# Channel stage of a four-layer convolution block: row-pair spectra, two-bank PSUM tiles and shorter Toeplitz rows

## The chip, the cores and the metric

The kernel runs on one core of one Trainium2 chip. The metric is device time of the whole launch in microseconds. All data are 32-bit floats; the trace shows each such matrix product as two instructions on TensorE (PE), each with a weight load of its own (PEld).

## The reference

The input x holds 32 images of 192 channels and 56 by 56 pixels. Four layers follow each other, each of the form x = x + layer(groupnorm(x)), with groups of 6 channels: an agent attention, a linear recurrence over the pixels (scan), a learned shift by whole pixels with a 3 by 3 filter, and a long convolution with a 55 by 55 filter for each channel. Cut to the two last ones, which the change touches:

```python
def _L2_conv_ref(inp, offset):          # a shift, then a separable 3x3 filter
    ...
    out = jax.vmap(shift_one, in_axes=(1, 0, 0, 0), out_axes=1)(x, yc, xc, mask)
    kern = jnp.exp(-sq / (2.0 * SIGMA ** 2))
    out_LO = jax.lax.conv_general_dilated(out, kern, ..., feature_group_count=Cn)

def _L3_conv_ref(x, z, ...):            # filter k from sines, then a long convolution
    ...
    y = jnp.fft.irfft2(jnp.fft.rfft2(x, s) * jnp.fft.rfft2(k[0], s)[None], s)
    y = y[..., Kh // 2:Kh // 2 + H, Kw // 2:Kw // 2 + W]
    return y + bias * x

x = x + _L2_conv_ref(_gn(x), L2_conv_offset)
x = x + _L3_conv_ref(_gn(x), ...)
```

## The kernel before, in words

`all_blocks` runs four parts in turn: `make_filter` (the long filter and its spectra along x, written to memory as `lags`), `attention` with `copy_spans` beside it (which lays the spectra out as `spans`), `scan_pairs`, and `channel_blocks`. Only the last, the channel stage, is touched.

The channel stage works on one channel at a time, all 32 images of it: a tile `x` has 112 used partitions, 56 image rows for each of two half batches that start at partitions 0 and 64, and 16 images by 56 columns along the free dimension. The steps of a channel c are:

- `load` (SP queue): two DMAs of x. `norm` (POOL): scale and shift of the first group norm; every fourth channel also builds the small matrices of the shift.
- `move_rows`, `move_columns` (PE): 8 products each, with the rows' and columns' matrices. Between them ACT copies the result into `across`; after them DVE adds it into x and sums it (`sums`).
- For a group of 6 channels `find_mean` and `find_spread` (small PE products), `keep_mean` (DVE). `centre` (DVE) and `square` (ACT), `sum_squares` (DVE) belong to a channel 6 behind c.
- `analyse` (PE), for a channel 12 behind: `_rows_to_spectra` multiplies 128 rows (both half batches) by `f1`, which holds cosines and sines for each half in a block of its own; 8 products of 168 columns, 3 to a PSUM tile. ACT copies the results to `y` in pieces of 64 partitions.
- `convolve` (PE): for each of 42 frequencies u, y against `toep`, the channel's Toeplitz matrix, 128 partitions by 56 by 84. Four products lie beside each other in 32-column strips of the array; 11 rounds of four make 44 products, the last two repeat u = 41. ACT writes the result into `turned`, scaled by the group's `rs`.
- `turn` (DVE): a transposition into `z`. `synthesise` (PE): 4 products with `back`. `finish` (DVE): two additions into `done`, and two DMAs on SP's queue to the output, in pieces of 224 bytes.
- `load_toeplitz` (ACT's queue): one DMA of 2352 KB, 128 partitions by 7 column groups of 2688 bytes each, asked for after `convolve` of channel b and meant for b + 3; there are three `toep` tiles.

The order is written out by hand in the loop at the end of `channel_blocks`. Each engine is wrapped in `_InOrder`, so every instruction of the stage carries the helper's line, L1546, in the profile, and stands on its engine in the order of the source. In one turn of the loop PE runs move_rows of channel c + 1, the group's mean and spread where they are due, analyse of b + 1, move_columns of c, synthesise of e = b - 1, and convolve of b, with b = c - 12. DVE's order in a turn is: the spreads' sums, turn (z), keep_mean, centre, the addition of move_columns, its sum, the addition of finish, the sum of squares. ACT's order is: the copy to across, the copies to y, square, the writes of turned, the issue of the Toeplitz load.

All PSUM tiles of the stage come from one pool of 8 tiles of one bank, taken in turn.

The scan, which is not changed, has two lines that the prediction uses: L921 multiplies by weights of 128 rows and L924 by weights of 64 rows, alternating between partitions 0 to 63 and 64 to 127:

```python
for h in range(len(outs[0])):
    for t, r in enumerate((slice(0, 64), slice(64, 128))):
        mm(outs[t][h], ca[r], srcs[2][h][r], start=False, stop=True)
```

Of the kernel before, what the change touches and what calls it, by code (L numbers as in the profile page):

```python
# [30 lines left out]
S = 56  # L31
# [1518 lines left out]
def channel_blocks(ctx: ExitStack, tc: tile.TileContext, taps, k, x2, rs2, spans, out):  # L1550
# [8 lines left out]
    nc = tc.nc  # L1559
    NB = out.shape[0]  # L1560
    NI, NG = NB // 2, NB // 4
    PX = 8 * S
    cp = ctx.enter_context(tc.tile_pool(name="d_c", bufs=1))
    wp = ctx.enter_context(tc.tile_pool(name="d_w", bufs=2))
    sp = ctx.enter_context(tc.tile_pool(name="d_s", bufs=2))
    pp = ctx.enter_context(tc.tile_pool(name="d_p", bufs=8, space=PSUM))
    pe, vector, scalar, pool, sync = (_InOrder(tc, e) for e in (nc.tensor, nc.vector, nc.scalar, nc.gpsimd, nc.sync))
    mm = pe.matmul

# [4 lines left out]
    pieces, at = [], 0  # L1574
# [80 lines left out]
    def load_toeplitz(c):  # L1655

        if not 0 <= c < C:
            return
        t = toep[c % len(toep)].rearrange("p j f -> p (j f)")
        n = S // SPAN  # L1660
        first = spans[c * n * 128]
        there = bass.AP(first.tensor, first.offset, [[FREQ, 128], [128 * FREQ, n], [1, SPAN * FREQ]])
        scalar.dma_start(out=t.rearrange("p (q f) -> p q f", q=n), in_=there)

    def move_rows(c):

        xn, rows = normed.pop(c).rearrange("p g w -> p (g w)"), made[c // 4][0]
        moved = across[c % len(across)]
        for i in range(0, NG, 4):
            ps = psum()  # L1670
            for g in range(4):
                mm(
                    ps[: 2 * S, g * 2 * S : (g + 1) * 2 * S], xn[:, (i + g) * 2 * S : (i + g + 1) * 2 * S], rows,
                    start=True, stop=True,
                )
            scalar.copy(
                moved[:, i : i + 4, :, 0:S].rearrange("p g s h -> p (g s) h"),
                ps[: 2 * S, :PX].rearrange("p (n h) -> p n h", h=S),
            )
        return moved  # L1680

    def move_columns(c, moved):

        n, j = divmod(c, GROUP)
        cols, x = made[c // 4][1], xs[c % len(xs)]
        flat = x.rearrange("p g w -> p (g w)")
        for i in range(2):
            ps = psum()
            for g in range(4):
# [22 lines left out]

    def find_mean(q):

        ps = psum()
# [8 lines left out]

    def find_spread(q):
        q.rs = sp.tile([128, 1], F32, name="rs", tag="rs")
        ps = psum()
# [16 lines left out]
        vector.tensor_reduce(groups[n].sums[:, 1, j], sq, AX.X, ALU.add)  # L1744

    def analyse(c):
        y = wp.tile([128, NI, 2, NF], F32, name="y", tag="y")
        _rows_to_spectra(pe, scalar, psum, padded[c % len(padded)], f1, y, NG)
        return y.rearrange("p g s u -> p (g s) u")

    def convolve(c, y):

        q, o, t = groups[c // GROUP], turned[c % len(turned)], toep[c % len(toep)]
        if c % GROUP < len(turned):
            vector.tensor_copy(o[0:32, :, SLOTS], q.fill.to_broadcast([32, S]))
        for a0 in range(0, QUAD, 4):
            n = min(4, QUAD - a0)
            ps = psum()
            for a in range(n):
                for i in range(4):  # L1760
                    u = min(4 * (a0 + a) + i, NF - 1)
                    mm(
                        ps[32 * i : 32 * i + 32, a * 2 * S : (a + 1) * 2 * S], y[:, :, u], t[:, :, 2 * u : 2 * u + 2],
                        start=True, stop=True,
                    )
            scalar.activation(
                o[:, :, 2 * a0 : 2 * (a0 + n)].rearrange("p j (a m) -> p a j m", m=2),
                ps[:, : n * 2 * S].rearrange("p (a j m) -> p a j m", a=n, m=2),
                AF.Copy, scale=q.rs,
            )  # L1770

    def turn(c):
        z = wp.tile([128, 32, S], F32, name="z", tag="z", bufs=1)
# [3 lines left out]
    def synthesise(c, z):  # L1777

        by = z.rearrange("p (g s) j -> p s g j", s=2)
        got = []  # L1780
        for i in range(2):
            ps = psum()
            for s in range(2):
                mm(
                    ps[HALF * s : HALF * s + HALF, :PX].rearrange("p (g w) -> p g w", w=S), back,
                    by[:, s, 8 * i : 8 * i + 8], start=True, stop=True,
                )
            got.append(ps[:, :PX].rearrange("p (g w) -> p g w", w=S))
        return got

    def finish(c, got):
        y = wp.tile([128, NI, S], F32, name="done", tag="done")
        t = padded[c % len(padded)][:, :, 0:S][:, :, ::-1]
        for i in range(2):
            g = slice(8 * i, 8 * i + 8)
            vector.tensor_tensor(y[:, g], t[:, g], got[i], ALU.add)
# [208 lines left out]
```

## Time and profile before

| | us |
|---|---|
| median of 3 timed runs | 10363.48 (10363.17 to 10363.57) |
| profiled execution | 10372.07 |
| its span, first to last instruction | 10370.2 |
| the channel stage in it | from about 8243 to 10370 |
| TensorE busy | 9436.8 (91%) |
| VectorE (DVE) busy | 9099.9 (88%) |
| ScalarE (ACT) busy | 6324.4 (61%) |

The page cuts the span into 40 slices and gives the busy tenths of each engine; the last 8 slices are the channel stage. Matrix products overlap in the pipeline, so a busy TensorE is not one at its peak, and how long a step takes is better read from start to start. The mean granted TensorE clock is 0.962 of full speed over the span and full in the steady part of the channel stage.

### The profile page before, as it was taken

Reading aid. Unit: us, or ns where it says so; the run is one execution under the profiler, and the core shown is the slowest. Engines: PE = TensorE matmul, PEld = TensorE weight load, DVE = VectorE, ACT = ScalarE, POOL = GpSimd, SP = SyncE. Lnnn points to the kernel's source line nnn. Section 1 sums busy time; section 2 is a strip of 40 time slices with the busy share of each in tenths; the row PEclk is TensorE's granted clock in tenths of the full one; section 3 lists DMA queues with packets and bytes.
Section 4 is the critical chain, followed back from the end, with each engine's and each line's share of the span. In section 5 each row is a group of like instructions: output and inputs, shape, how many; then the busy total and the mean of one; then the engine's idle time right before and its main releaser. Section 6 shows DMA issues by size and latency. Waiting matters only on the chain. (4 is left out here: it accounts for less than half of the span.)

```text
span 10370.2 us, 162899 instructions
## 1 busy us (share of the span) xinstructions
PE 9436.8 (91%) x63814; PEld 5816.8 (56%) x63814; DVE 9099.9 (88%) x11284; ACT 6324.4 (61%) x11964; POOL 2223.2 (21%) x1751
## 2 busy tenths in 40 slices
PE   5999999999999999998888888888888799999998
PEld 3555555655565555555333343333334488888886
DVE  5888888888888888887999999999999788888887
ACT  3555555555555555554566666666666567777777
POOL 0000000000000000000333333333333354554442
PEclk9999999999999999998899999999999899999999
DMA  4212221122112211111244444344444489999999
GB/s 129 68 37 66 68 68 44 58 68 68 47 55 68 68 46 29 49 49 43 69 107 101 103 103 105 104 104 101 101 101 101 129 247 303 307 306 304 304 304 278
DMA packets 1111096, 1247.61 MB, mean 120 GB/s; under 512 B 773091, under 2 KB 813440, under 8 KB 1098232
## 3 DMA queue, kind: packets, MB, share of 16 engines
q1 hardware_dynamic: 914284, 746.65, 28.1%
q10 hardware_dynamic: 196036, 490.46, 13.9%
q8 instruction: 506, 8.29, 0.3%
q14 instruction: 270, 2.21, 0.1%
HBM read 916.15 MB, written 306.43 MB: 118 GB/s over the span
## 5 line engine op out<-in xcount | busy, mean ns | idle before, releaser
L649 DVE SCALAR_TENSOR_TENSOR o<-v_a,att_w,o 128x896 f32<-128x896 f32 (+1 forms) x1024 | 1056.8, 1032 | 422.2 <-ACT v_a L623 301.9
L1167 POOL MEMSET f<- 128x2 f32 x48 | 4.5, 99 | 4751.2 <-DMA st_c<-st 4748.8
L1546 DVE STREAM_TRANSPOSE z<-turned 128x1792 f32<-128x1792 f32 x192 | 680.3, 3543 | 211.2 <-ACT turned L1546 211.2
L1546 ACT COPY y<-ps 64x252 f32<-64x252 f32 (+1 forms) x2304 | 784.6, 341 | 89.6 <-PE ps L1546 59.8
L1161 ACT ACTIVATE pq<-pq 128x784 f32<-128x784 f32 x384 | 329.4, 858 | 676.6 <-DVE pq L1157 676.4
L1153 DVE TENSOR_TENSOR_SCAN pq<-decay,f,both 128x784 f32<-128x784 f32 x384 | 695.7, 1841 | 9.1 <-ACT both L1183 9.1
L1157 DVE SCALAR_TENSOR_TENSOR pq<-both,eu,pq 128x1568 f32<-128x1568 f32 x384 | 701.3, 1840 | 2.0 <-POOL f L1156 0.4
L666 ACT ACTIVATE pr<-ps,low 98x896 f32<-98x896 f32 (+1 forms) x384 | 352.3, 918 | 572.7 <-DVE low L664 572.7
L1153 DVE TENSOR_TENSOR_SCAN pq<-decay,b,both 128x784 f32<-128x784 f32 x384 | 694.1, 1839 | 0.0
L921 PE MATMUL ps<-x,weights 128*128 128x392 f32 x1536 | 584.6, 519 | 83.4 <-ACT x L1141 54.2
L649 DVE SCALAR_TENSOR_TENSOR o<-v_c,att_w,o 128x448 f32<-128x448 f32 (+1 forms) x1024 | 638.6, 624 | 4.9
L662 PE MATMUL ps<-xs_a,gk_a 128*98 128x448 f32 (+1 forms) x1536 | 636.8, 495 | 0.0
L776 ACT ACTIVATE pq<-pq 128x1176 f32<-128x1176 f32 (+2 forms) x224 | 241.9, 1080 | 642.5 <-DVE pq L768 620.5
L663 PE MATMUL ps<-xs_c,gk_c 125*98 125x448 f32 (+1 forms) x1536 | 631.3, 492 | 0.0
L1141 ACT ACTIVATE x<-x,nb,rs 128x784 f32<-128x784 f32 x384 | 386.5, 1030 | 337.3 <-DMA x<-x 183.2
L1546 PEld LDWEIGHTS ps<-toep,y 128*32 128x32 f32 x16896 | 500.4, 151 | 160.9 <-issue 76.0
L763 PE MATMUL ps<-gq_a,xs_a 128*128 128x294 f32 (+1 forms) x1600 | 547.0, 425 | 37.7 <-DVE pq L768 33.1
L1546 PE MATMUL ps<-toep,y 128*32 128x112 f32 x16896 | 560.5, 286 | 12.6 <-DVE done L1546 11.1
L1156 POOL COPY b<-pq 128x2 f32<-128x2 f32 x192 | 394.7, 2056 | 660.9 <-DVE pq L1153 567.3
L1546 POOL TENSOR_TENSOR xn<-x,scale 128x896 f32<-128x896 f32 x192 | 329.7, 1717 | 937.4 <-DMA x<-x 670.5
L764 PE MATMUL ps<-gq_c,xs_c 125*128 125x294 f32 (+1 forms) x1600 | 519.9, 413 | 0.0
L1546 ACT ACTIVATE turned<-ps,rs 128x448 f32<-128x448 f32 (+1 forms) x576 | 377.3, 663 | 223.3 <-PE ps L1546 216.0
(360 smaller groups left out, 23488.2 us busy)
## 6 DMA issues: line engine op xcount, KB each, us to landing
toep<-spans ACTq DMA_DIRECT2D x192, 2352.0 KB
x<-x SPq DMA_DIRECT2D x576, 392.0 KB
x<-x SPq DMA_DIRECT2D x896, 196.0 KB
out_x<-done SPq DMA_DIRECT2D x384, 196.0 KB
spans<-lags SPq DMA_DIRECT2D x24, 2352.0 KB
x<-in_x SPq DMA_DIRECT2D x32, 1568.0 KB
x<-x SPq DMA_DIRECT2D x32, 1568.0 KB
gq_c<-once SPq DMA_DIRECT2D x32, 821.1 KB
```

Source lines behind the costliest of these rows:

```text
L649: nc.vector.scalar_tensor_tensor(dst, tap(i), dww[:, t, i : i + 1], dst, ALU.mult, ALU.add)
L662: mm(ps[P2, h, :n], g[:, cols], xs_a[j][:, px], start=True, stop=False)
L663: mm(ps[P2, h, :n], gk_c[0:KC, 2 * j + h, cols], xs_c[j][0:KC, px], start=False, stop=True)
L666: nc.scalar.activation(pr[:, :, :n], ps[P2, :, :n], AF.Exp, bias=low[:, j, p : p + 1], accum_out=sums[:, j, p : p + 1])
L763: mm(ps[:m, k - q, :HA], xs_a[j][:, px], g, start=True, stop=False)
L764: mm(ps[:m, k - q, :HA], xs_c[j][0:KC, px], gq_c[0:KC, which[k]], start=False, stop=True)
L921: mm(out, aa, srcs[t][h], start=True, stop=False)
L1141: nc.scalar.activation(xs[t], xs[t], AF.Identity, bias=nb1[:, t, s.p : s.p + 1], scale=rs1[:, t, s.p : s.p + 1])
L1153: nc.vector.tensor_tensor_scan(to, decay[:, of(t)].to_broadcast([128, MC]), data, at[:, i : i + 1], ALU.mult, ALU.add)
L1156: nc.gpsimd.tensor_copy(at, z[:, :, last])
L1157: nc.vector.scalar_tensor_tensor(before, both, eu[:, of(t)], before, ALU.mult, ALU.add)
L1546: return lambda *args, **kw: self.tc.keep_in_program_order(do(*args, **kw))
```

## The change

Five things change in `channel_blocks`:

1. `analyse` no longer calls `_rows_to_spectra`. For each of the 8 image pairs it makes two products of 64 rows, one for each half batch, of 84 columns, into two banks of one tile. Six pairs go into a first tile and two into a second; ACT copies 56 partitions at a time.
2. All PSUM tiles are two banks wide, and there are 4 of them. The results of move_rows, move_columns and synthesise lie in one tile each, and ACT or DVE reads both banks in one instruction. convolve has two tiles (64 and 20 instructions on PE).
3. convolve makes 42 products and not 44; move_columns uses 120 of 128 weight columns.
4. `load_toeplitz` fetches the three middle column groups as before, on ACT's queue, and the outer four in four DMAs on SP's queue, 48 partitions and 5376 bytes each. The rows left out are zeros, written once.
5. `toep`, `y` and `turned` are zeroed in part at the start of the stage.

```diff
+    ROWS = HALF + S
-    pp = ctx.enter_context(tc.tile_pool(name="d_p", bufs=8, space=PSUM))
+    pp = ctx.enter_context(tc.tile_pool(name="d_p", bufs=4, space=PSUM))
...
+    EDGE = 8
+    for t in toep:
+        for p in (0, HALF):
+            nc.vector.memset(t[p : p + 32, 0 : 2 * SPAN], 0.0)
+            nc.vector.memset(t[p + 32 : p + 64, 0 : 2 * SPAN], 0.0)
+            nc.vector.memset(t[p + 32 : p + 64, 5 * SPAN :], 0.0)
...
+        nc.vector.memset(t[64:128, :, SLOTS - 2 : SLOTS], 0.0)
+    ys = kept("y", [128, NI, 2, NF], 2)
+    for t in ys:
+        nc.vector.memset(t, 0.0)
...
-        return pp.tile([128, BANK], F32, name="ps", tag="ps")
+        return pp.tile([128, 2, BANK], F32, name="ps", tag="ps")
...
-        there = bass.AP(first.tensor, first.offset, [[FREQ, 128], [128 * FREQ, n], [1, SPAN * FREQ]])
-        scalar.dma_start(out=t.rearrange("p (q f) -> p q f", q=n), in_=there)
+        there = bass.AP(
+            first.tensor, first.offset + 2 * 128 * FREQ, [[FREQ, 128], [128 * FREQ, 3], [1, SPAN * FREQ]]
+        )
+        scalar.dma_start(out=t.rearrange("p (q f) -> p q f", q=n)[:, 2:5], in_=there)
+        for q, p, to in ((1, EDGE, 0), (5, 0, 5)):
+            for m in range(2):
+                there = bass.AP(
+                    first.tensor, first.offset + (q * 128 + m * HALF) * FREQ, [[FREQ, S - EDGE], [1, 2 * SPAN * FREQ]]
+                )
+                at = HALF * m + p
+                sync.dma_start(out=t[at : at + S - EDGE, to * SPAN * FREQ : (to + 2) * SPAN * FREQ], in_=there)
...
-        for i in range(2):
-            ps = psum()
-            for g in range(4):
-                mm(ps[:, g * 2 * S : (g + 1) * 2 * S], moved[:, 4 * i + g].rearrange("p s h -> p (s h)"), cols[: 2 * S], start=True, stop=True)
-            px = slice(i * PX, (i + 1) * PX)
-            vector.tensor_tensor(flat[:, px], flat[:, px], ps[:, :PX], ALU.add)
+        ps = psum()
+        for g in range(NG):
+            mm(
+                ps[:ROWS, g // 4, g % 4 * 2 * S : (g % 4 + 1) * 2 * S],
+                moved[:, g].rearrange("p s h -> p (s h)")[:, :ROWS], cols[: 2 * S], start=True, stop=True,
+            )
+        there = x[:ROWS].rearrange("p (b g) w -> p b (g w)", b=2)
+        vector.tensor_tensor(there, there, ps[:ROWS, :, :PX], ALU.add)
...
-        y = wp.tile([128, NI, 2, NF], F32, name="y", tag="y")
-        _rows_to_spectra(pe, scalar, psum, padded[c % len(padded)], f1, y, NG)
+        y, flat = ys[c % len(ys)], padded[c % len(padded)].rearrange("p g w -> p (g w)")
+        for g0, n in ((0, 6), (6, 2)):
+            ps = psum()
+            for g in range(n):
+                at = (g0 + g) * 128
+                for s in range(2):
+                    r = slice(HALF * s, HALF * s + HALF)
+                    mm(
+                        ps[:ROWS, s, g * FREQ : (g + 1) * FREQ], flat[r, at : at + ROWS],
+                        f1[r, s * FREQ : (s + 1) * FREQ], start=True, stop=True,
+                    )
+            got = ps[:, :, : n * FREQ].rearrange("p s (g m u) -> p s g m u", m=2, u=NF)
+            for i in range(2):
+                for m in range(2):
+                    scalar.copy(
+                        y[HALF * m : HALF * m + S, 2 * g0 + i : 2 * (g0 + n) : 2].rearrange("p g s u -> p s g u"),
+                        got[HALF * i : HALF * i + S, :, :, m],
+                    )
...
-        for a0 in range(0, QUAD, 4):
-            n = min(4, QUAD - a0)
+        for a0, n in ((0, 8), (8, QUAD - 8)):
             ps = psum()
             for a in range(n):
-                for i in range(4):
-                    u = min(4 * (a0 + a) + i, NF - 1)
+                for i in range(min(4, NF - 4 * (a0 + a))):
+                    u = 4 * (a0 + a) + i
...
+            for p, part in ((128, slice(0, n - 1)), (64, slice(n - 1, n))):
+                scalar.activation(
+                    o[:p, :, 16:SLOTS].rearrange("p j (a m) -> p a j m", m=2)[:, part],
+                    ps[:p, 0, : n * 2 * S].rearrange("p (a j m) -> p a j m", a=n, m=2)[:, part],
+                    AF.Copy, scale=q.rs[:p],
+                )
```

move_rows, synthesise and finish change in the same way as move_columns: one tile, one copy or addition over both banks. The first eight rounds of convolve are written to `turned` in one instruction of ACT.

More of the change, by code (lines that the diff above doesn't have):

```diff
@@ L1668, in move_rows @@
         moved = across[c % len(across)]
-        for i in range(0, NG, 4):
-            ps = psum()
-            for g in range(4):
[L1672 to L1678, printed above, removed]
-            )
+        ps = psum()
+        for g in range(NG):
+            mm(
+                ps[: 2 * S, g // 4, g % 4 * 2 * S : (g % 4 + 1) * 2 * S], xn[:, g * 2 * S : (g + 1) * 2 * S], rows,
+                start=True, stop=True,
+            )
+        scalar.copy(
+            moved[:, :, :, 0:S].rearrange("p (b g) s h -> p b (g s) h", b=2),
+            ps[: 2 * S, :, :PX].rearrange("p b (n h) -> p b n h", h=S),
+        )
         return moved
@@ L1685, in move_columns @@
         cols, x = made[c // 4][1], xs[c % len(xs)]
-        flat = x.rearrange("p g w -> p (g w)")
-        for i in range(2):
-            ps = psum()
-            for g in range(4):
-                mm(ps[:, g * 2 * S : (g + 1) * 2 * S], moved[:, 4 * i + g].rearrange("p s h -> p (s h)"), cols[: 2 * S], start=True, stop=True)
-            px = slice(i * PX, (i + 1) * PX)
-            vector.tensor_tensor(flat[:, px], flat[:, px], ps[:, :PX], ALU.add)
+        ps = psum()
+        for g in range(NG):
+            mm(
[4 more added lines that the diff above has]
+        vector.tensor_tensor(there, there, ps[:ROWS, :, :PX], ALU.add)
         if j == 0:
@@ L1713, in find_mean @@
     def find_mean(q):
-        ps = psum()
+        ps = psum()[:, 0]
         mm(ps[:, :NI], ones, q.total, start=True, stop=True)
@@ L1726, in find_spread @@
         q.rs = sp.tile([128, 1], F32, name="rs", tag="rs")
-        ps = psum()
+        ps = psum()[:, 0]
         for i in range(4):
@@ L1746, in analyse @@
     def analyse(c):
-        y = wp.tile([128, NI, 2, NF], F32, name="y", tag="y")
-        _rows_to_spectra(pe, scalar, psum, padded[c % len(padded)], f1, y, NG)
+        y, flat = ys[c % len(ys)], padded[c % len(padded)].rearrange("p g w -> p (g w)")
+        for g0, n in ((0, 6), (6, 2)):
+            ps = psum()
+            for g in range(n):
+                at = (g0 + g) * 128
+                for s in range(2):
+                    r = slice(HALF * s, HALF * s + HALF)
+                    mm(
+                        ps[:ROWS, s, g * FREQ : (g + 1) * FREQ], flat[r, at : at + ROWS],
[4 more added lines that the diff above has]
+                for m in range(2):
+                    scalar.copy(
+                        y[HALF * m : HALF * m + S, 2 * g0 + i : 2 * (g0 + n) : 2].rearrange("p g s u -> p s g u"),
+                        got[HALF * i : HALF * i + S, :, :, m],
+                    )
         return y.rearrange("p g s u -> p (g s) u")
@@ L1755, in convolve @@
             vector.tensor_copy(o[0:32, :, SLOTS], q.fill.to_broadcast([32, S]))
-        for a0 in range(0, QUAD, 4):
-            n = min(4, QUAD - a0)
+        for a0, n in ((0, 8), (8, QUAD - 8)):
             ps = psum()
             for a in range(n):
-                for i in range(4):
-                    u = min(4 * (a0 + a) + i, NF - 1)
-                    mm(
-                        ps[32 * i : 32 * i + 32, a * 2 * S : (a + 1) * 2 * S], y[:, :, u], t[:, :, 2 * u : 2 * u + 2],
-                        start=True, stop=True,
-                    )
[L1766 to L1770, printed above, removed]
+                for i in range(min(4, NF - 4 * (a0 + a))):
+                    u = 4 * (a0 + a) + i
+                    mm(
+                        ps[32 * i : 32 * i + 32, a // 4, a % 4 * 2 * S : (a % 4 + 1) * 2 * S], y[:, :, u],
+                        t[:, :, 2 * u : 2 * u + 2], start=True, stop=True,
+                    )
+            if a0 == 0:
+                scalar.activation(
+                    o[:, :, 0:16].rearrange("p j (b a m) -> p b a j m", b=2, m=2),
+                    ps[:, :, :PX].rearrange("p b (a j m) -> p b a j m", a=4, m=2),
+                    AF.Copy, scale=q.rs,
+                )
+                continue
+            for p, part in ((128, slice(0, n - 1)), (64, slice(n - 1, n))):
+                scalar.activation(
+                    o[:p, :, 16:SLOTS].rearrange("p j (a m) -> p a j m", m=2)[:, part],
+                    ps[:p, 0, : n * 2 * S].rearrange("p (a j m) -> p a j m", a=n, m=2)[:, part],
+                    AF.Copy, scale=q.rs[:p],
+                )
     def turn(c):
@@ L1779, in synthesise @@
         by = z.rearrange("p (g s) j -> p s g j", s=2)
-        got = []
+        ps = psum()
         for i in range(2):
-            ps = psum()
             for s in range(2):
                 mm(
-                    ps[HALF * s : HALF * s + HALF, :PX].rearrange("p (g w) -> p g w", w=S), back,
+                    ps[HALF * s : HALF * s + HALF, i, :PX].rearrange("p (g w) -> p g w", w=S), back,
                     by[:, s, 8 * i : 8 * i + 8], start=True, stop=True,
                 )
-            got.append(ps[:, :PX].rearrange("p (g w) -> p g w", w=S))
-        return got
+        return ps[:, :, :PX].rearrange("p b (g w) -> p b g w", w=S)
     def finish(c, got):
@@ L1793, in finish @@
         t = padded[c % len(padded)][:, :, 0:S][:, :, ::-1]
-        for i in range(2):
-            g = slice(8 * i, 8 * i + 8)
-            vector.tensor_tensor(y[:, g], t[:, g], got[i], ALU.add)
+        vector.tensor_tensor(
+            y.rearrange("p (b g) w -> p b g w", b=2), t.rearrange("p (b g) w -> p b g w", b=2), got, ALU.add
+        )
         for s in range(2):
```

## The prediction

> **What bounds it now.** I read the slices of the page first: the edit touches only the last stage, from 8243 us to the end, and there DVE, PE and DMA are all near full. The windows view of 400 us of that stage gives the totals (columns: stretch, length, busy PE, weight loads, DVE, ACT, POOL, granted clock, DMA share, GB/s), and the DMA view of the same stretch splits the DMA share by queue (q10 carries ACT's issues, the Toeplitz loads; q1 carries SP's).
>
> ```profile
> 9200.00:9600.00 400.00, 394.52 (x5483) 335.25 (x5483) 349.81 (x352) 306.64 (x696) 200.58 (x175) 1.00 1.02 306
> q10 hardware_dynamic: 34510, 91.13, 65.9%
> q1 hardware_dynamic: 75345, 30.42, 35.3%
> ```
>
> The groups count 38 transposes in it, so a channel takes 400/38 = 10.53 us: DVE works 9.2, ACT 8.1, DMA 10.7 by the sum of its packets. Which of PE and DMA sets the pace? The timeline of PE tells it (start, length, instructions): a group's first channel, then an ordinary one.
>
> ```profile
> 9291.33 1.20 PE L1546 MATMUL ps<-toep,y 128*32 128x112 f32 x32
> ...
> 9301.85 1.72 PE L1546 MATMUL ps<-z,fixed 128*64 128x448 f32 x8 [0.83 <-DVE x L1546]
> 9303.50 2.86 PE L1546 MATMUL ps<-toep,y 128*32 128x112 f32 x88
> 9306.29 1.82 PE L1546 MATMUL ps<-rows,xn 128*112 128x112 f32 x16
> 9307.95 2.46 PE L1546 MATMUL ps<-fixed,padded 128*128 128x168 f32 x16
> 9310.25 1.94 PE L1546 MATMUL ps<-cols,across 112*128 112x112 f32 x16
> 9312.11 1.73 PE L1546 MATMUL ps<-z,fixed 128*64 128x448 f32 x8
> 9313.77 2.52 PE L1546 MATMUL ps<-toep,y 128*32 128x112 f32 x76
> ```
>
> From start to start the ordinary channel costs: convolve 2.79, move_rows 1.66, analyse 2.30, move_columns 1.86, synthesise 1.66: 10.27 us with no wait between them. Over the stage five channels of six take 10.27 to 10.4; the group's first takes 11.3 to 12.7 (here 12.17), for DVE is late and PE waits for its PSUM. So TensorE is the bound of the ordinary channel. The Toeplitz load asked for after convolve of channel b is for b+3 and in the trace lands some 12 us after its issue; no PE wait in the waits view names it. DMA is the second limit, close behind.
>
> **PE, step by step.** Analyse swaps 8 products of 128 rows by 168 columns (two instructions each, 16 in all, 142 ns apart) for 16 products of 64 rows by 84 columns, in pairs on the two halves of the array's rows. Nothing in this stage does that, but the scan's L924 does, between full products of L921 (PEld is the weight load):
>
> ```profile
> 8217.01 0.96 PEld L924 LDWEIGHTS ps<-sq,fixed 64*128 64x128 f32 x8 [0.56 <-issue]
> 8217.01 1.59 PE L924 MATMUL ps<-sq,fixed 64*128 64x392 f32 x8
> 8218.53 2.27 PEld L921 LDWEIGHTS ps<-y,wogs 128*128 128x128 f32 x8 [0.56 <-issue]
> 8218.53 2.90 PE L921 MATMUL ps<-y,wogs 128*128 128x392 f32 x8
> 8221.36 0.96 PEld L924 LDWEIGHTS ps<-y,wogs 64*128 64x128 f32 x8 [0.56 <-issue]
> ```
>
> Start to start, 8 full ones take 2.83 and 8 half ones 1.52. If halves run two at a time, 8s + w = 2.83 and 4s + w = 1.52, so a step s is 0.33 us (392 columns) and a change of shape w is 0.21 us; the loads' busy time falls by the same half, so they overlap too. In analyse a pair streams only 84 columns, half of today's 142 ns, so the load of 120 columns will set the step: 112-column loads go 98 ns apart (1.66/16 with its change of shape), 128-column loads in move_columns 111. I take 104 ns. Analyse: 16 x 0.104 = 1.66, plus 0.21 at each end, which today's neighbours of equal shape don't pay: 2.08 instead of 2.30.
>
> [...]
>
> Move_columns loads 120 columns for 128: 16 x 7 ns = 0.10 less, 1.76. Convolve drops two repeated products (88 instructions to 84, 2.79/22 = 0.127 per four; the last fours become half-filled and save less): 0.05 less, 2.74. Move_rows and synthesise keep their instructions. Sum: 1.66 + 2.08 + 1.76 + 1.66 + 2.74 = 9.90, so 0.37 us less per ordinary channel. Bounds: pairs at 98 and no drain, 0.9 less; pairs at 208, nothing overlapped, 1.3 more.
>
> **ACT and DVE.** Rows of ACT in the groups of the same stretch (after the count: busy us, mean ns of one; then the idle time before):
>
> ```profile
> L1546 ACT COPY y<-ps 64x252 f32<-64x252 f32 x304 | 110.6, 364 | 14.6 <-PE ps L1546 11.1
> L1546 ACT ACTIVATE turned<-ps,rs 128x448 f32<-128x448 f32 x76 | 54.0, 718 | 39.9 <-PE ps L1546 39.1
> L1546 ACT COPY y<-ps 64x168 f32<-64x168 f32 x152 | 44.7, 294 | 2.2
> L1546 ACT ACTIVATE turned<-ps,rs 128x336 f32<-128x336 f32 x38 | 21.2, 559 | 0.5
> ```
>
> Copies of y cost 0.83 ns an element and 0.15 us each: 12 (4.1 us) become four of 504 (0.57) and four of 168, 3.5 us. The turned writes cost 1.42 ns an element and 0.08 each: 2.0 us becomes 1.35 + 0.40 + 0.24, the same; but the first can now start only after 64 of 84 products, so the last ends about 1.3 us after convolve instead of 0.6. The transposition z (3.55) starts then; it ends 7.65 us after convolve's start, and synthesise is due at 2.74 + 1.66 + 2.08 + 1.76 = 8.2. It stays hidden, with 0.6 us of slack where there were 1.6. DVE's two pairs of additions become two single ones and save two fixed costs, 0.3 us: 8.9 of 9.9. So nothing here lengthens the ordinary channel; if this cover goes, each 0.1 us late is 15 us in all.
>
> PSUM has 4 double tiles for 8 single ones. In ordinary channels each tile is read long before its turn. In a group's first channel it isn't: in the order rows, mean, spread, analyse (two), columns, move_columns takes the tile of the mean, which keep_mean frees after z on DVE, about 8 us after convolve's start, and move_columns would be due at 2.74 + 1.66 + 0.45 + 2.08 = 6.9. I price this at 1.2 us beside what those channels lose today (12.17 against 10.27 + 0.45 for their own products), partly the same wait: a group channel goes from 12.0 to 12.2.
>
> **DMA and the queues.** Today a channel costs 65.9% of 10.53 = 6.94 on q10 and 3.72 on q1. Three of seven column groups stay on ACT, 2.97; the outer four carry 48 of 64 rows, 3/7 of the bytes, 2.97 at the same rate and maybe a sixth more or less in pieces of twice the length. Sum 9.7 (9.2 to 10.2) with the small queues, under 9.9 but not by much. The four new DMAs stand on SP behind out and ahead of the next x loads, and wait for the end of convolve; x then goes out some 3 us later. Behind it wait only POOL's norm and, two channels on, move_rows; the waits view has POOL idle for x 117 us of 400, so there is slack. In the built program a DMA waits for the DMA eight before it; with nine a channel for five, the fourth new one waits for the same channel's x load, issued some 8.5 us before (9.9 less the issues between): free while that lands in time.
>
> **Ends.** At the start 18 memsets of 1344 elements on DVE (0.94 ns an element by the memset of turned) take 23 us, where DVE was idle to 8270 us; SP's x loads of the next channels stand behind the Toeplitz pieces that wait for them: +5 (0 to 12). At the end 12 channels run by a loop that the chain of waits shows, z, synthesise, convolve, the turned writes, z:
>
> ```profile
> 10268.89 3.51 DVE z L1546
> ...
> 10277.62 3.51 DVE z L1546
> ```
>
> 8.73 us a turn; the later turned writes add 0.65: +8.
>
> **Sum.** About 179 full channels: 149 ordinary x -0.37 = -55; 30 group channels x +0.2 = +6; start +5; end +8: -36 us. The profiled execution spans 10370.2 (10372.07 with what lies around it), so its span would be 10334; the median of the timed runs, 10363.48, becomes 10327. Low end: no drain paid, and DMA, at 9.5, stops the gain at 0.75 a channel: 149 x -0.75 + 8 = -104, 10260.
>
> **Rivals.** *DMA becomes the bound* (0.15): pieces of 5376 bytes at the rate of q1's worst, 10.2 us a channel, or the eight-deep wait costing as much. Against it: bytes fall by 14%. Saving 0.1 or less, eaten by start and end: 10345 to 10385, no change. *The half-row loads go one after another* (0.13): place analyse, price 16 x 0.104 more, ordinary channel 11.57, 179 x 1.3 less the 1.2 us of waits that group channels would hide, 10570. It decides from 127 ns a pair on, where the saving is gone. Against it L924; for it, that L924 is bound by streams of 392 columns and never shows loads alone setting the pace. *The slack of 0.6 before synthesise goes* (0.07): z late by 0.7 us and more in each channel, 10385 to 10450. The forecast has the other 0.65.
>
> So faster by over 0.2% (21 us, about what a measurement here can tell) 0.65, within it 0.15, slower 0.20. The range, 10260 to 10410, leaves out most of the serial case and little else.
>
> **What would show it.** Right: in PE's timeline analyse starts 2.1 us before move_columns, convolve to convolve 9.9 us; the DMA share stays near 0.98 at less GB/s; group channels near 12. Wrong: analyse at 3 us or more (loads serial); idle before synthesise released by z; PE waiting for toep or xn; SP waiting on x loads with the engines idle.

## The result, and the profile after

| | before | after |
|---|---|---|
| median, us | 10363.33 (10355.80 to 10363.57, 4 runs) | 11092.42 (11079.29 to 11102.46, 4 runs) |
| ratio, 95% interval | | 1.0705 (1.0686 to 1.0723) |
| profiled execution: its time, its span | 10372.07, 10370.2 | 11102.46, 11100.3 |
| mean of a turn, first 179 turns | 10.605 | 14.381 |
| mean of a turn, last 12 | 8.93 | 11.39 |

The change made the kernel 7% slower; the forecast was 0.35% faster. A turn is measured from one start of convolve to the next; a full one serves one channel. The 179 full turns lost 676 us, the last twelve 29.5, and the first convolve came 24 us later: together the 730 us between the two spans.

The same stretch of the channel stage in the windows view, and its two large queues in the DMA view (columns as before):

```profile
9200.00:9600.00 400.00, 312.08 (x4314) 263.80 (x4314) 248.78 (x204) 191.68 (x365) 137.21 (x122) 0.87 0.87 199
q1 hardware_dynamic: 60538, 49.88, 59.4%
q10 hardware_dynamic: 11200, 28.90, 26.5%
```

No engine is full any more: TensorE went from 394 busy us to 312, with fewer instructions and at a granted clock of 0.87. The DMA engines move 199 GB/s, not 306, yet their packets fill 0.87 of the time. So either many bytes move slowly or the issuing queues stand still. PE's timeline, an ordinary channel and the start of the next:

```profile
9532.80 3.33 PE L1546 MATMUL ps<-rows,xn 128*112 128x112 f32 x16 [3.58 <-POOL xn L1546]
9536.06 2.90 PE L1546 MATMUL ps<-fixed,padded 64*120 64x84 f32 x32
9538.89 1.93 PE L1546 MATMUL ps<-cols,across 112*120 112x112 f32 x16
9540.75 1.72 PE L1546 MATMUL ps<-z,fixed 128*64 128x448 f32 x8
9542.41 2.79 PE L1546 MATMUL ps<-toep,y 128*32 128x112 f32 x84
9548.58 3.33 PE L1546 MATMUL ps<-rows,xn 128*112 128x112 f32 x16 [3.38 <-POOL xn L1546]
```

Once started, the steps are about as short as forecast (columns 1.86, synthesise 1.66 from start to start; analyse 2.83 in this turn, with the clock still low, and 1.84 in the next). But ahead of move_rows TensorE waits 3.4 to 3.6 us for xn, and the rows then take 3.26 us for 1.66: after such a wait the granted clock is low (0.87 in the mean of the stretch above; the last turns, below, show how). The waits view, 9200 to 10000 us, follows it back, and the waits of SyncE's own queue (SPq) end the search (columns: total us, number of waits, longest):

```profile
POOL xn L1546 <- DMA x<-x: 329.4, 36, 13.8
PEld ps L1546 <- POOL xn L1546: 175.7, 49, 8.3
PE ps L1546 <- POOL xn L1546: 164.0, 47, 8.1
```

```profile
SPq L1546 <- DMA toep<-spans: 474.7, 68, 11.7
```

So xn waits for x, and x is late because SyncE, which should ask for it, stands behind Toeplitz loads for 475 of 800 us. With 56 channels in the 800 us, PE's wait is 2.9 us a channel; with 9.83 of work (the channel of a later run without waits) and 1.5 by which the steps are slower here in the mean of all turns (move_rows 0.8, analyse 0.4, move_columns 0.2, synthesise 0.1) that makes 14.3 of the 14.4.

ScalarE's groups (count, busy us, mean ns) came out as priced: y in pieces of 0.575 and 0.294, turned in 1.042, 0.438 and 0.340, 1.82 us in all against 2.0 forecast.

```profile
L1546 ACT COPY y<-ps 56x504 f32<-56x504 f32 x108 | 62.1, 575 | 24.0 <-PE ps L1546 22.0
L1546 ACT ACTIVATE turned<-ps,rs 128x896 f32<-128x896 f32 x28 | 29.2, 1042 | 47.4 <-PE ps L1546 47.4
```

### The profile page after: what moved, and what is told of

Read it like the earlier page. It is cut to its first block, busy times and chain, and to the rows that moved or that the text cites. A ratio compares the mean times of both kernels' runs of the same rounds, so it can differ in the third digit from the quotient of the medians.

```text
span 11100.3 us, 167943 instructions
## 1 busy us (share of the span) xinstructions
PE 9674.9 (87%) x66118; PEld 5983.6 (54%) x66118; DVE 9086.3 (82%) x10922; ACT 6117.5 (55%) x11004; POOL 2172.8 (20%) x1751
## 5 line engine op out<-in xcount | busy, mean ns | idle before, releaser
L1546 PE MATMUL ps<-rows,xn 128*112 128x112 f32 x3072 | 489.7, 333 | 536.8 <-POOL xn L1546 509.9
L1546 DVE TENSOR_TENSOR x<-x,ps 120x896 f32<-120x896 f32 x192 | 208.7, 1087 | 729.1 <-issue 475.8
L1546 ACT COPY y<-ps 56x504 f32<-56x504 f32 (+1 forms) x1536 | 668.0, 435 | 206.3 <-PE ps L1546 173.7
L1546 PEld LDWEIGHTS ps<-rows,xn 128*112 128x112 f32 x3072 | 447.3, 239 | 578.7 <-POOL xn L1546 573.6
L1546 ACT COPY across<-ps 112x896 f32<-112x896 f32 x192 | 174.0, 906 | 842.4 <-PE ps L1546 813.0
```

The source lines that it names most:

```text
L1546: return lambda *args, **kw: self.tc.keep_in_program_order(do(*args, **kw))
```

## First experiments: one part at a time

**The products and tiles without the pieces**: the change, with the old single Toeplitz load.

```diff
-        scalar.dma_start(out=t...[:, 2:5], in_=there)     # three groups
-        for q, p, to in ((1, EDGE, 0), (5, 0, 5)): ...    # four pieces
+        scalar.dma_start(out=t.rearrange("p (q f) -> p q f", q=n), in_=there)
```

> The changed kernel with the Toeplitz load of before: one DMA of 2352 KB a channel on ACT's queue, no zeroing of toep; half-row analyse, two-bank tiles and 42 products stay. Theory S (slots): the loss comes from SP's DMAs, which stand in a rotation of eight slots with nine DMAs a channel, so that an x load (or the DMA just ahead of it) waits each channel for the landing of the Toeplitz load on ACT's queue, 9 us after its issue. Rival D (rate): the pieces of 48 partitions by 5376 bytes move slowly (0.39 us a packet in the changed kernel). Rival O (order): the pieces stand on SP ahead of the x loads and wait for convolve's end. All three expect the loss gone here and the PE part alone: 10290 to 10370, convolve to convolve 9.9 to 10.5 us. Rival P (PE and PSUM part slower than priced) expects 10500 or more.

Measured: 10727.08, ratio 1.0348 (1.0330 to 1.0365), and an ordinary channel of 12.4 us. PE's timeline names two waits a channel:

```profile
9528.60 1.72 PE L1546 MATMUL ps<-z,fixed 128*64 128x448 f32 x8 [1.24 <-DVE x L1546]
9531.98 2.79 PE L1546 MATMUL ps<-toep,y 128*32 128x112 f32 x84 [1.65 <-DVE done L1546]
```

Synthesise reads z, so why does it wait for VectorE's addition into x? That can only be about its PSUM tile. In this program as built, 149 of 192 synthesise get the very tile that move_columns has just filled (one use back), and one part of convolve (121 of them) gets the one that synthesise has just filled. In the changed kernel as built it is not so: there the same 149 get the tile of move_rows, four uses back, and none that of move_columns. The pool does not hand out in turn, and an edit of the loads changed what it handed out. So this run blames the products for a loss that the change does not have.

**The pieces without the products**: the kernel before, with the change's Toeplitz loads and zeros.

> The kernel before with the new Toeplitz load and its zeroing alone; analyse, tiles and products as before. S, D and O all expect nearly the whole loss: 10950 to 11150, about 14.5 us a channel, and SP waiting for Toeplitz loads. Rival P expects 10450 or less.

Measured: 11095.76, ratio 1.0704 (1.0686 to 1.0721); SyncE waits 467.8 us for toep. The pieces alone cost as much as the whole change.

**The pieces on ScalarE's queue** (`sync.dma_start` to `scalar.dma_start` for the four), and **all loads on SyncE's** (the large one moved there too):

> The changed kernel with the four pieces issued on ACT's queue, behind the large Toeplitz load, in place of SP's. Bytes and pieces are the same, nine DMAs a channel. S: the DMA eight after the large load is then one of the next channel's stores or loads, a whole channel later, and no x load waits for a fresh Toeplitz load: 10320 to 10450. O: x is no longer behind the pieces: 10320 to 10400. D: the pieces are as slow as ever: 10950 or more.

> The changed kernel with the large Toeplitz load on SP's queue too, so that all nine DMAs of a channel stand in one queue in one order. S: the DMA eight after the large load is a store of the next channel, which comes a channel later, so nothing waits for a fresh landing: 10330 to 10480. O: x still stands behind all pieces and convolve's end: 10950 or more. D: 10950 or more.

Measured: 10976.03, ratio 1.0579 (1.0561 to 1.0597), and 10720.71, ratio 1.0330 (1.0306 to 1.0353). The first tells little: its program has the poor tiles too (149 of 192), and ScalarE waits 81 us of 800 for toep. The second halves the loss: SyncE's waits for toep fall to 229 us of 800. But it meets a second limit: the DMA share is 1.00 at 234 GB/s. The time lies between two of the ranges that were expected; of the theories, D had named slow pieces.

## The tiles made fast

Each of the four double tiles gets a name of its own, handed out strictly in turn.

```diff
-        return pp.tile([128, 2, BANK], F32, name="ps", tag="ps")
+        turns[0] += 1
+        return pp.tile([128, 2, BANK], F32, name="ps", tag=f"ps{turns[0] % 4}")
```

> The pairs and double tiles with the old single Toeplitz load, as in the run with one load (10727 us), but the four double PSUM tiles are handed out strictly in turn, each with a name of its own. Theory T (tiles: in the run with one load, synthesise was given the very tile that move_columns had just filled, and the second part of convolve the one that synthesise had just filled, so TensorE waited for VectorE twice a channel): the ordinary channel goes from 12.4 us to 9.9 to 10.5, and the time to 10290 to 10420 us; the waits of TensorE for x and for done vanish. Rival W (work: VectorE and ScalarE are simply late with longer instructions, whichever tile is used): no better than 10650 us, the waits stay under other names.

> The whole change with the four double tiles handed out strictly in turn, nothing else. Theory S (slots: nine DMAs a channel on eight rotating semaphores make SyncE stand behind the large Toeplitz load in most turns, and this loop of 29 us for two channels sets the pace): it stays at 10950 to 11100 us, SyncE's waits for toep near half of its time. Rival T alone (the tiles are the main loss and the late loads follow from it): 10700 us or less.

> The whole change with the large Toeplitz load on SyncE's queue as well (10721 us in the earlier run), and the four double tiles handed out strictly in turn. If S and T are the whole loss: an ordinary channel of 9.9 to 10.5 us, 10290 to 10450 us. Rival B (bytes: the pieces of 5376 bytes cost the DMA engines more time than the rows of 2688 that they replace, 12.4 us a channel at a share of 1.00): no better than 10650 us, with the DMA share at 1.00 and TensorE waiting for xn.

The products with the old load: 10308.94, ratio 0.9948 (0.9932 to 0.9965), faster than before. The whole change: 11099.32, ratio 1.0707 (1.0689 to 1.0725), as it was; its tiles were nearly in turn already (a few came three, five or six uses back). All on SyncE: 10723.18, ratio 1.0339 (1.0320 to 1.0359), as without the names; here the rival of its expectation came true, the DMA share at 1.00 and TensorE waiting for xn. PE's timeline of the first, an ordinary channel:

```profile
9512.42 2.79 PE L1546 MATMUL ps<-toep,y 128*32 128x112 f32 x84
9515.13 1.82 PE L1546 MATMUL ps<-rows,xn 128*112 128x112 f32 x16
9516.89 1.91 PE L1546 MATMUL ps<-fixed,padded 64*120 64x84 f32 x32
9518.73 1.93 PE L1546 MATMUL ps<-cols,across 112*120 112x112 f32 x16
9520.59 1.72 PE L1546 MATMUL ps<-z,fixed 128*64 128x448 f32 x8
9522.25 2.80 PE L1546 MATMUL ps<-toep,y 128*32 128x112 f32 x84
```

Convolve to convolve 9.83 us, no wait: the prediction's 9.90 for TensorE, and for this part its time.

## Why the pieces are slow

A packet is the part of a DMA that goes to one partition in one stretch of bytes: in the DMA records of after a piece has 48 of 5376 bytes, the large load 384 of 2688. The mean packet of a piece, 5376 bytes, took 387 ns in the change and 405 with all loads on SyncE: 13 to 14 bytes per ns. The old load's 2688 bytes took 124 ns before: 21.6.

**Length and overlap.** Two runs on top of the last one: each piece read as two parts of 2688 bytes a row from the old load's places, and each piece read from rows 5376 bytes apart. The second brings other values into the tile, so it measures time only and is no usable kernel.

```diff
-first.offset + (q * 128 + m * HALF) * FREQ, [[FREQ, S - EDGE], [1, 2 * SPAN * FREQ]]
+first.offset + (to * 128 + at) * FREQ, [[FREQ, S - EDGE], [128 * FREQ, 2], [1, SPAN * FREQ]]
```

```diff
-first.offset + (q * 128 + m * HALF) * FREQ, [[FREQ, S - EDGE], [1, 2 * SPAN * FREQ]]
+first.offset + m * HALF * FREQ, [[2 * SPAN * FREQ, S - EDGE], [1, 2 * SPAN * FREQ]]
```

> As the run with all loads on SyncE and the tiles in turn (10723 us), but each of the four pieces is read as two parts of 2688 bytes a row from the two places that the old load read, in place of one part of 5376 bytes from one place: same bytes, same 48 rows, same number of DMAs. Theory L (the long reads are the slow ones; whether by their length or because 48 rows that start 336 bytes apart read the same few kilobytes, stays open here): a short part takes 110 to 150 ns as those of the old load do, the DMA share falls below 1.00, the ordinary channel comes to 9.8 to 10.2 us, 10270 to 10400 us. Rival R (48 rows for 128 are the reason: fewer partitions take the bytes more slowly, whatever the length): a short part takes 190 ns or more, 10650 us or more.

> As the run with all loads on SyncE and the tiles in turn (10723 us), but the rows of a piece start 5376 bytes apart in DRAM for 336, so that no two read the same bytes; length, rows and DMAs stay (the outer groups' values are then other rows of the same channel). Theory O (overlap: the rows of a piece read the same few kilobytes and wait for each other): a piece's part of 5376 bytes falls from 400 ns to 215 to 260, 10270 to 10400 us. Rivals L by length alone and R (48 rows): the part stays at 350 ns or more, 10650 us or more.

Measured: 10724.06, ratio 1.0338 (1.0321 to 1.0356), and 10705.85, ratio 1.0323 (1.0306 to 1.0340). The large load's 2688 bytes took 136 ns before these edits; in the first run the mean over its packets and the pieces', in equal numbers, is 168.5, which leaves 201 for a piece's, again 13.4 bytes per ns. In the second a part still takes 384. Neither the length nor the overlap in memory is the reason.

**Rows.** As many bytes, in as many DMAs on the same queue, but on 128 partitions by 2016 bytes. Here too the outer groups get other values, part of them zeros, so the time alone counts:

```diff
-        for q, p, to in ((1, EDGE, 0), (5, 0, 5)): ...
+        for i in range(4):
+            n = 6 * FREQ
+            there = bass.AP(first.tensor, first.offset + (4 + i // 2) * 128 * FREQ, [[FREQ, 128], [1, n]])
+            sync.dma_start(out=t[:, (5 * SPAN if i > 1 else 0) * FREQ + i % 2 * n :][:, :n], in_=there)
```

> As the run with all loads on SyncE and the tiles in turn (10723 us), but the four pieces of 48 rows by 5376 bytes become four of 128 rows by 2016 bytes: same bytes, same number of DMAs, same queue (the outer groups then hold other values, and part of them zeros). Rival R (few rows: 48 neighbouring partitions take the bytes at about half the rate of 128): the DMA engines' rate rises from 234 to 290 GB/s or more, the ordinary channel falls from 12.3 us to 9.8 to 10.3, 10270 to 10400 us. Theory N (it is the number of DMAs, or their all standing on one queue): 10650 us or more.

Measured: 10319.00, ratio 0.9955 (0.9938 to 0.9971); 2016 bytes take 86 ns, 23.3 per ns. The windows of the run with the 48-row pieces and of this one, both with all loads on SyncE and the tiles in turn:

```profile
9200.00:9600.00 400.00, 348.33 (x5054) 290.91 (x5052) 291.54 (x232) 224.03 (x425) 163.91 (x144) 0.91 1.00 229
```

```profile
9200.00:9600.00 400.00, 391.30 (x6084) 326.21 (x6082) 362.53 (x287) 272.60 (x520) 205.86 (x168) 0.98 0.95 280
```

Equal bytes a channel, 229 against 280 GB/s, a turn of 12.3 us against 10.2. So the pieces are slow because each reaches only 48 neighbouring partitions. Whether it is their number that counts, or that all lie in one half of 64, these runs don't separate. x's loads have 56 rows, also in one half, and moved 18.7 bytes per ns before and 20.2 with the products alone, so the number of rows does not give the rate by itself. In the run with all rows the DMA rate stayed a little under the 290 that was expected, with TensorE near full.

In the run with the 48-row pieces the packets of the pieces fill 154 of the 400 us, 4.75 us a channel. Why a DMA into so few partitions goes slowly is in no trace here.

**Both halves at once.** Of each pair of pieces, one on each queue (`(sync, scalar)[m].dma_start`):

> As the run with all loads on SyncE and the tiles in turn (10723 us), but of each pair of pieces the one for partitions below 64 stays on SyncE's queue and the one for partitions above goes out on ScalarE's, so that both halves can be written at once. If R holds, the parts of 5376 bytes fall from 400 ns to 220 to 320 and the time to 10300 to 10550 us, unless ScalarE is held by the rotation of the semaphores as in the earlier run with all pieces on it (its waits for toep would show that). Under N: 350 ns or more, 10650 us or more.

Measured: 11121.76, ratio 1.0732 (1.0714 to 1.0750), and the parts took 458 and 430 ns: the hoped-for gain did not come. SyncE again stood behind Toeplitz loads for 489 of 800 us, so the run does not tell the halves alone, and no other run shows such a pair by itself.

## Why the queue stands

A semaphore is a counter; the traces list which one each DMA raises when it lands. In the traces of before and after the DMAs of SyncE and ScalarE take eight of them in rotation, and from 8400 us on none is issued before the one ahead of it on its semaphore has landed (950 pairs before, 1710 after). Matched to their landings in the trace of after, 146 x loads follow a large Toeplitz load on their semaphore, and 145 of these were issued within 0.15 us of its landing; before, at most 3 of some 340 x loads were held by any DMA. SyncE's timeline (start and length of each group of issues) shows one such turn:

```profile
9498.20 3.66 SPq L1546 DMA_DIRECT2D toep<-spans  x4
9501.96 8.29 SPq L1546 DMA_DIRECT2D x<-x  x2
9510.35 1.56 SPq L1546 DMA_DIRECT2D scale<-rs  x2
9512.01 1.23 SPq L1546 DMA_DIRECT2D out_x<-done  x2
9513.34 11.00 SPq L1546 DMA_DIRECT2D toep<-spans  x4
```

The first x load goes out at 9501.96, the second only at 9509.94, 0.02 us after the large load that ScalarE had asked for at 9498.82. Everything behind it on SyncE, the outputs and the next pieces, is late by as much. This is the queueing; what does it cost without slow rows, and without bytes?

> As the run with pieces of 128 rows by 2016 bytes and all loads on SyncE (10319 us), but the large Toeplitz load back on ScalarE's queue, so that the nine DMAs a channel take the eight semaphores in the order of the change (the outer groups hold other values, part of them zeros, as there). If the rotation is dear by itself, whatever the loads take: SyncE stands behind the large load for half of its time as in the change, 10600 us or more. If it is dear only because the 48-row pieces make the large load land late (some 9.5 us after its issue): it lands in 6 to 8 us here, SyncE's waits for toep stay under a quarter of its time, 10310 to 10420 us.

> The kernel before, with four DMAs of 48 rows by 8 numbers a channel on SyncE, after the large Toeplitz load, into scratch that nothing reads; they wait for nothing but the rotation of the DMA semaphores. The full Toeplitz load stays (this adds work to the kernel). Theory S: nine DMAs a channel on eight semaphores are enough, SyncE stands behind the large load: 10800 us or more. Rival B: bytes and packets matter, 192 short packets a channel are nothing: 10360 to 10450 us.

With pieces of 128 rows (again for the time only) and the large load on ScalarE: 10649.28, ratio 1.0267 (1.0245 to 1.0290). The large load lands in 7.5 us on average, about 8 where it holds another, and still SyncE waits:

```profile
SPq L1546 <- DMA toep<-spans: 385.9, 79, 13.1
```

These waits aren't the change's, though: in this program the outputs (81 of 146 held) and the scale loads (22 of 27) follow the large load, and the x loads don't. With four tiny loads added to the kernel before (there the order on the semaphores is another): 10491.57, ratio 1.0121 (1.0104 to 1.0138), under a third of what was expected; the waits fell mostly on outputs and on the large load itself. So the price depends on who follows whom: with the products alone 142 x loads follow a large load too, but it lands in time for all but 3. With all loads on SyncE it is the outputs that follow the large load, and the waits are short where the pieces have 128 rows (22 of 146 held, against 136 of 147 with 48 rows). The two causes side by side, tiles in turn in all four:

| median, us | all loads on SyncE | large load on ScalarE |
|---|---|---|
| pieces of 128 rows, as many bytes of other values | 10319.00 | 10649.28 |
| pieces of 48 rows, as in the change | 10723.18 | 11099.32 |

The rows cost 404 and 450, the large load on a second queue 330 and 376: two causes of like size. That they nearly add up is no more than a sum, since the two programs on the right hold different loads behind the large one. Without both the change is where the products alone are, at 10308.94.

## The last turns, and the fastest version

In the run of the products with the old load, a turn of the last twelve takes 10.7 us for 8.93, not the 0.65 more of the prediction. Synthesise takes 2.0 to 3.2 us there (median 2.9), after waits of 2.8 to 2.9 for z; before, it takes 1.72 after waits of 1.7 to 2.0. Two tries to end the writes of turned earlier, both with convolve's short tile first: by single banks of the two-bank tile, and with all PSUM in eight single-bank tiles in turn.

```diff
+                if a0 == 0 and a % 4 == 3:
+                    scalar.activation(o[:, :, 2 * a - 6 : 2 * a + 2]..., ps[:, a // 4, :PX]..., AF.Copy, scale=q.rs)
```

```diff
-        return pp.tile([128, 2, BANK], F32, name="ps", tag=f"ps{turns[0] % 4}")
+        return pp.tile([128, BANK], F32, name="ps", tag=f"ps{turns[0] % 8}")
-            ps = psum()                    # analyse: both halves in one tile
+            both = [psum(), psum()]
-        for a0, n in ((0, 8), (8, QUAD - 8)):
+        for a0, n in ((8, QUAD - 8), (0, 4), (4, 4)):
```

> The pairs and the tiles in turn with the old single Toeplitz load (10309 us), but convolve fills its short tile first and the two-bank tile last, and ScalarE writes turned by single banks. Theory: the last write then ends 0.8 us after convolve for 1.2 to 1.3; in the last turns of the stage TensorE waits less than the 2.9 us for z and synthesise keeps 1.7 us for 2.5 to 3.2, so a turn there takes 9.0 to 9.3 us for 10.7: 15 to 20 us less, 10285 to 10295 us; the ordinary channel stays at 9.83. Rival: the short synthesise of the last turns has another reason than the wait before it, and only 0.4 us a turn is won, 5 us in all, 10304 us.

> The pairs of half-row products and the shorter convolve with the old single Toeplitz load, but in eight single-bank tiles handed out in turn (two tiles for the two halves of a pair), so turned is again written by banks, without the wait of 0.8 us that a second bank of one tile brought. Theory: ordinary channel 9.83 as with the double tiles in turn, the last turns of the stage 9.0 us for 10.7, 10280 to 10295 us. Rival: with 8 copies of y more and two additions more per channel ScalarE (8.1 us a channel) or VectorE (9.2) come late in every channel: 10350 us or more.

The first: 10495.28, ratio 1.0115 (1.0098 to 1.0132). Here the writes to the second bank of the tile wait for the reading of the first (0.78 us in one turn, 0.85 in the next); PE's timeline has it in the middle of convolve, every channel, which costs 1.06 us a turn (the ordinary channels with single-bank tiles have no wait there):

```profile
9516.77 1.85 PE L1546 MATMUL ps<-toep,y 128*32 128x112 f32 x52
9519.47 1.18 PE L1546 MATMUL ps<-toep,y 128*32 128x112 f32 x32 [0.85 <-ACT turned L1546]
```

The second: 10292.90, ratio 0.9926 (0.9910 to 0.9943), within the expected range but not for the expected reason: the last turns still take 10.4 us, not 9.0, and the gain is in the groups' first channels, 10.7 for 11.9 in its profile. In the last turns TensorE still waits 2.6 to 2.75 us and synthesise takes 3.1. Is that the clock? Idle products into a tile that nothing reads fill the wait, nine of them and then two:

```diff
+        if within(e) and not within(c):
+            idle = psum()
+            for _ in range(9):             # then: range(2)
+                mm(idle[:HALF, :PX], back, fixed[:, 0:PX], start=True, stop=True)
```

> The fastest kernel so far (single banks in turn, 10293 us), and in the last turns of the stage, where TensorE waits 2.6 to 2.8 us for z, nine products of 448 columns into a tile that nothing reads, about 1.9 us, ahead of synthesise. Theory: synthesise takes 3.1 us there instead of 1.7 because the granted clock falls after the wait; with the wait cut to 0.8 us it takes 1.7, a turn 9.0 us for 10.4, and the time falls by 13 to 19 us to 10275 to 10281 us. Rival: synthesise is slow there for another reason (PSUM or the reads of z): 10290 us or more.

> As the run with the filled wait (10330 us), with two products for nine: these take 0.75 us each, so that nine filled 6.8 us, over twice the wait of 2.7; two fill 1.5. Theory of the granted clock: synthesise takes 1.7 us in the last turns, TensorE is idle there for no more than 1.3 us at a stretch, a turn takes 8.9 to 9.2 us for 10.4, and the time is 10270 to 10281 us. Rival: a wait this short does not matter and synthesise stays at 3.1 us, 10290 us or more.  The two versions differ by 15 us at most, which five rounds may not tell apart by the time alone; the turn and the length of synthesise in the trace decide.

Nine: 10329.85, ratio 0.9964 (0.9951 to 0.9976), slower than without; they took 6.8 us where 1.9 had been reckoned, and a turn 13.0, but synthesise was back at 1.7. Two: 10276.65, ratio 0.9924 (0.9910 to 0.9938), a turn 9.06, PE in the last turns:

```profile
10200.87 1.72 PE L1546 MATMUL ps<-fixed 128*64 128x448 f32 x4
10203.51 1.72 PE L1546 MATMUL ps<-z,fixed 128*64 128x448 f32 x8 [0.92 <-DVE z L1546]
```

So the wait itself slowed the next step. The granted clock in the last turns is 1.00 before, 0.84 with the products in turn and 0.99 here. The 0.84 is a mean of two speeds; the run of the products in turn, from the end of one wait on:

```profile
10213.48:10216.90 3.42, 0.77 (x4) 0.34 (x6) 3.42 (x2) 3.02 (x8) 0.00 (x0) 1.00 0.95 304
10216.90:10220.31 3.41, 3.41 (x43) 1.96 (x43) 1.70 (x3) 0.95 (x1) 0.00 (x0) 0.50 0.85 339
```

TensorE ends a wait of 2.8 us at 10216.13, works 0.77 us at full clock, and then 3.41 us at half. In the traces of before and after the clock is 1.00 or 0.50, in stretches of 3.41 us or whole multiples of it (all but the last of 256 stretches and of 474). The waits for xn of the changed kernel (8400 to 10960 us) show which waits are enough: of 60 under 1.5 us none was followed by slow rows, of 46 from 1.5 to 3.4 us 30 were, and all 69 longer ones. What parts the middle ones is not shown. Of the two fastest versions, whose intervals overlap, the turns tell the difference, not the medians.

## Why the prediction was wrong

*TensorE's steps: right in the mechanism, and in the sum partly by luck.* 9.90 us forecast, 9.83 measured where nothing else bounds, but the misses cancel in part. Analyse took 1.84 (2.08 forecast, between bounds): the pairs overlap as L924 had shown (115 ns a pair, where the bound for pairs that don't was 208). If a pair takes the 104 ns assumed, which no run shows by itself, 0.09 us is left for each change of shape (the "drain" of the forecast's bounds), not 0.21, though part of it may stand in move_rows (1.76 for 1.66). Move_columns gained nothing from 120 columns (1.86 for 1.76).

*PSUM: right for the change, by luck.* Each tile is indeed free long before its turn in the changed kernel as built, and a group's first channel takes 11.9 us (12.2 forecast) in the products-alone run. But that four tiles go round in turn was assumed. Even the eight of the kernel before do not, as built: 207 of 384 of synthesise's tiles there come two or three uses after move_columns had them. And the first experiment shows a neighbouring program where they don't, at 418 us (10727.08 less 10308.94).

*DMA time, 9.7 us a channel: wrong, and the first step that failed.* Its term "2.97 at the same rate and maybe a sixth more or less" for the outer groups measured 4.75: 14% fewer bytes of the load took longer to move. That is with all loads on SyncE, where x and the outputs bring the sum to 12.3; in the changed kernel the pieces took 4.55. A row at hand pointed that way: x, with 56 partitions of 3584 bytes a DMA, moved 18.7 bytes per ns against 21.6 of the load with 128. The prediction priced it as a cost of q1 and not of the rows, though no run here shows which it is for x.

*The queue, "the fourth new one waits for the same channel's x load", "free while that lands in time": wrong, and the second.* What it says of that pair came true: of 202 pieces that follow an x load none was held. The pair it left out was the dear one: an x load follows a large Toeplitz load that was asked for less than a turn earlier, and waits for it in 145 of 146 cases. The text counted the order in the source on one queue; the semaphores go round over two queues, in the order of the built program. The "slack" of POOL was real, 117 us of 400, but SyncE lost 7.0 us at a time on average and up to 11.7.

*The rival "DMA becomes the bound"* named both places, at 10.2 us a channel and 10345 to 10385 us; they measured 12.3 (the rows, all loads on SyncE), 12.1 (128 rows, the large load on ScalarE) and 14.4 us a channel (both). *The half loads in series* and *the slack before synthesise* did not happen. Of the prediction's signs of error the trace shows PE waiting for xn, and SyncE waiting with the engines idle, though for the large load and not for an x load.

*The ends.* The last turns: +0.65 us a turn forecast, +1.8 measured with the products alone; in the single-bank version filling the wait took 1.3 us off a turn (10.36 to 9.06), so the miss is mostly the clock after a longer wait. The start: +5 forecast, the first convolve 24 us later in this profile but 4 us earlier in the run with names; left open.

## What to carry to other kernels

Before a load is cut to fewer rows, ask how many partitions each piece reaches: with 14% fewer bytes the Toeplitz load took 7.97 us a channel of the DMA engines (3.22 + 4.75) for 6.94. Before DMAs are added, write down for each which DMA it follows on its semaphore in the built program, over all queues, and when that lands; here slow loads ahead of small urgent ones held the whole issuing queue, 7.0 us at a time on average. And when one part of a change is tried alone, look which buffers the built program gave it: the first trial here was slower for a reason that the change itself did not have.

## What the runs showed of the hardware

- DMAs into 48 neighbouring partitions ran at 11.7 to 14.0 bytes per ns and engine, in parts of 2688 or 5376 bytes and with source rows close or spaced (the lowest where one of each pair stood on a second queue); DMAs into 128 at 20.0 to 23.3 in the runs without such pieces, and at 17.1 to 19.8 beside them.
- A DMA share of 1.00 is no bound by itself: it stood beside 318 GB/s with TensorE full (products alone) and beside 229 with TensorE waiting.
- DMAs issued by two engines wait for each other through shared semaphores: 145 of 146 x loads of SyncE that follow a large load went out, in the trace of after, within 0.15 us of the landing of that load, which ScalarE had issued.
- The granted clock of TensorE is 1.00 or 0.50 in the traces of before and after, in stretches of 3.41 us or multiples of it. After waits under 1.5 us the next 1.7 us of work was never slowed in the changed kernel, after 1.5 to 3.4 us in 30 of 46 turns, and after longer ones always, to 3.3 us. Two products of 0.75 us that nobody needs, put in the wait, gave back 1.3 us a turn.
